# Layer 3's second weights: the third product by quarter blocks too, from the seventh group on, and statistics and first sums placed behind the third's sums

## The chip, the cores and the metric

The kernel runs on one core of one Trainium2 chip. The metric is the device time of one execution in microseconds (us); lower is better. The median of three runs stands for a kernel.

## The reference, cut to what matters

The whole model is four graph layers with a pre-layernorm and a residual on 8192 tokens of width 256 (128 samples of 64 nodes). The change lies in the last one:

```python
# --- layer 3 ---
h = jnp.maximum(_layernorm(x, axis=-1), 0.0)
S = adj
def _slconv(x, adj, S, W):
    support = jnp.einsum('bnf,fh->bnh', x, W)
    return jnp.einsum('nm,bmh->bnh', adj * S, support)
h = relu(_slconv(h, adj, S, W1))   # 256 -> 512
h = relu(_slconv(h, adj, S, W2))   # 512 -> 1024
x = x + _slconv(h, adj, S, W3)     # 1024 -> 256
```

Everything is in float32.

## The kernel before

**Layer 3 by groups.** The tokens are cut into 16 groups of 512 (GT = 4 tiles of 128). For each group g the loop at the end of the kernel goes through these stages: layernorm and the first mixing over the nodes (done ahead, during the group before), `first_weights` (matmuls at L1700), `second_mix` (L146), `second_weights` (L1772 and L197), `third_weights` (L1824), `last_mix` (L1845) and `finish`, which adds to the residual and stores. The stages of neighbouring groups interleave: the last mix of group g-1 and the mixing for g+1 lie between the first and second weights of g. The order of the instructions on each engine is fixed when the program is built; `tc.issue_after(ins)` puts what it traces behind `ins` on the engine of `ins`. Each engine works through its own queue in order, and waits at the head of it.

**Products by seven.** Each weight stage multiplies 2x2 blocks with seven products in place of eight (`seven`): sums of one operand's blocks (`sums`, L339), differences of the other's (`differences`, L327), then products 1, 5, 7, 6 into four PSUM banks. ACT copies products 1 and 5 out (p1, p5; L256), DVE adds 7 and 6, and products 2, 3 and 4 are accumulated into banks that are already in use. The four result blocks are: `out[0][0]` = products 1 + 2; `out[1][1]` = p1 + p5, added by POOL (`last_sum`, L267); `out[0][1]` = p1 + ps[5] with product 3 accumulated into ps[5] (`sum_of_three`, L272); `out[1][0]` = p1 + ps[7] with product 4 accumulated (`sum_of_four`, L278). `end` applies the relu (L350, ACT).

**The second weights** run `seven` in two passes, q = 0 and q = 2, each for two of the four 128-wide column blocks. One product there is four matmuls of 128x128 weights on 256 columns.

**Quarter blocks.** From the fifth group on (`SPLIT_FROM = 4`) products 6 and 2 of both passes are themselves done by seven products of quarter blocks, each one matmul of 128 columns (class `Split`): `first` issues four (1, 5, 7, 6) into the four quarters of one bank, `common` takes them out, `last` accumulates the other three, and `rest` adds three quarters to the target. `common` is

```python
nc.scalar.copy(self.u, q[0])                      # L207, ACT
for k in (1, 2):
    nc.vector.tensor_tensor(t[3], t[3], q[k], ALU.add)          # L209, DVE
summed = nc.vector.tensor_tensor(self.u, self.u, q[3], ALU.add) # L210, DVE
nc.gpsimd.tensor_tensor(out=three, in0=three, in1=self.u...)    # L213, POOL
```

with `u` a 128x128 scratch block in a freed residual tile, one for each split product and shared by the two passes. `rest` is L223 (DVE, 128x384). `split_second` makes the sums of the weights' quarter blocks once, after the fourth group's second weights; `split_differences` (L231) makes those of the activations in each group.

**The order around the change.** The two passes first issue products 1, 5, 7 and the first part of 6 each. Then `half` of pass 1, `half` of pass 2 (product 3, the last part of 6, the first part of 2, and their additions), then `other_half` of each (last part of 2, product 4). The third's sums (L339, four of 128x512 for each of q = 0 and 2) follow on DVE, tied behind `parts_summed` entries (the L210 instructions). The statistics of the group after next (`ln_scale`: L93 to L99, with one POOL instruction at L97) are tied behind the last of the second's differences, that is, they come near the start of the second weights; the next group's first sums (L339, four of 128x256) are free to follow them. What needs the statistics is the rectification on ACT (L112) during the next group's first weights; what needs the first sums is the fifth product there (L1700).

**Tiles.** `arena(ar_right)` hands out eight tiles in rotation; one group uses eight of them.

Of the kernel before, what the change touches and what calls it, by code (L numbers as in the profile page):

```python
# [15 lines left out]
P = 128  # L16
D = 256
# [22 lines left out]
def adj_preln_kernel(ctx: ExitStack, tc: tile.TileContext, x_in, adj, vec, bg0, bg1,  # L40
# [200 lines left out]
    def seven(products, banks, p1, p5, out, end, parts=lambda b: [b], split=None,  # L241
              order=(1, 5, 6, 7)):

        ps = dict(zip(order, banks))
        for i in (1, 5, 7, 6) if split else order:
            if split and i == 6:  # L250
                split[6].first(ps[6])
            else:
                products[i](ps[i], True)
        for i in order:
            if i in (1, 5):
                copied = nc.scalar.copy(p1 if i == 1 else p5, ps[i])  # L256
        if split:
            added = nc.vector.tensor_tensor(p5, p5, ps[7], ALU.add)
            split[6].common(ps[6], p1)
            nc.scalar.copy(out[0][0], ps[1])  # L260
        else:
            nc.vector.tensor_tensor(p1, p1, ps[6], ALU.add)
            added = nc.vector.tensor_tensor(p5, p5, ps[7], ALU.add)  # L263

        def last_sum():
            sums_on_pool.append(
                nc.gpsimd.tensor_tensor(out=out[1][1], in0=p1, in1=p5, op=ALU.add).ins  # L267
            )
            end(1, 1, None)

        def sum_of_three():
            nc.vector.tensor_tensor(out[0][1], p1, ps[5], ALU.add)  # L272
            end(0, 1, None)

        def sum_of_four():
            products[4](ps[7], False)
            for to, p, q in zip(*(parts(b) for b in (out[1][0], p1, ps[7]))):
                last = nc.vector.tensor_tensor(to, p, q, ALU.add)  # L278
                end(1, 0, None, to)
            return last.ins  # L280

        def half():
            products[3](ps[5], False)
            split[6].last(ps[6])
            split[6].rest(ps[6], p1)
            last_sum()
            split[2].first(ps[1])
            split[2].common(ps[1], out[0][0])
            sum_of_three()

        def last_half():
            split[2].last(ps[1])
            split[2].rest(ps[1], out[0][0])
            end(0, 0, None)

        def finish():
            if split:
                half()
                last = sum_of_four()
                last_half()  # L300
                return last
            last_sum()
            products[2](ps[1], False)
            end(0, 0, ps[1])
            products[3](ps[5], False)
            sum_of_three()
            return sum_of_four()

        def other_half():
            last_half()  # L310
            sum_of_four()

        finish.halves = (half, other_half) if split else (finish,)
        finish.behind = added.ins
        finish.copied = copied.ins
        return finish
# [13 lines left out]
    def sums(eng, a11, a12, a21, a22, s1, s2, s3, s4, behind=None, which=range(4)):  # L330

        ops = (
            (s1, a21, a22, ALU.add), (s2, s1, a11, ALU.subtract),
            (s3, a11, a21, ALU.subtract), (s4, a12, s2, ALU.subtract),
        )
        for i in which:
            s, p, q, op = ops[i]
            with each_behind(behind, i):
                last = eng.tensor_tensor(out=s, in0=p, in1=q, op=op)  # L339
        return last.ins  # L340
# [629 lines left out]
    def arena(pool):  # L970
        return pool.tile([P, 4, GN], F32, tag="arena", name="arena")
# [715 lines left out]
        )  # L1687
        return a, lambda: add_back(2, pss[2])

    def first_weights(a, room, copied):  # L1690

        h1 = arena(ar_left)
        act = [[a[:, 2 + c, m * HN : (m + 1) * HN] for c in range(2)] for m in range(2)]
        ss = [a[:, i // 2, (i % 2) * HN : (i % 2 + 1) * HN] for i in range(4)]
        summed = sums(nc.vector, *act[0], *act[1], *ss)

        def product(w, b):
            def issue(ps, first):
                for t in range(2):
                    nc.tensor.matmul(  # L1700
                        ps[:, t, :], lhsT=w[:, t * P : (t + 1) * P], rhs=b,
                        start=first and t == 0, stop=True, skip_group_check=True,
                    )

            return issue

        p1, p5 = (room[:, i, :].rearrange("p (t f) -> p t f", t=2) for i in (2, 3))
        blocks = [[h1[:, 2 * m : 2 * m + 2, n * D : (n + 1) * D] for n in range(2)] for m in range(2)]
        end = seven(
            sevens((*act, ss), (*b1, t1s), product), [bank((P, 2, D)) for _ in range(4)], p1, p5,  # L1710
            blocks, ends_in(blocks, AF.Relu),
        )
        with tc.issue_after(end.copied):
            next_a = copied()
        end()
        return h1, summed, next_a
# [6 lines left out]
            order=[(2, (2, 3, 0, 1)), (0, range(GT))],  # L1723
        )

    def split_second():

        free = [xpool.tile([P, GT, D], F32, tag=f"x{g}", name=f"free{g}") for g in range(3)]
        quarters = {}
        for i, a, s in ((6, s2s[1], free[0]), (2, a2[0][1], free[1])):  # L1730
            rows = a.rearrange("p c (q r f) -> p c r q f", r=2, f=P)
            blocks = [[rows[:, c, r] for c in range(2)] for r in range(2)]
            s = s.rearrange("p a (i f) -> p a i f", f=P)
            split_sums(nc.vector, blocks, s)
            quarters[i] = blocks, s
        return free[2], quarters

    def second_weights(m1, room, within=None):

# [9 lines left out]
        ts = [tt[:, i] for i in range(4)]  # L1749
        last = differences(nc.vector, *act[0], *act[1], *ts)  # L1750
        if within:
            small = within[0].rearrange("p a (i n) -> p (a i) n", n=P)
            tb = {
                6: split_differences(nc.vector, ts[1], small[:, 0:3]),
                2: split_differences(nc.vector, act[1][0], small[:, 3:6]),
            }

        def split(k):
            if not within:
                return None  # L1760
            return {
                i: Split(split_weights(*within[1][i], k), tb[i], small[:, 6 + i // 6])
                for i in (2, 6)
            }

        def products(q):
# [16 lines left out]
        for q in (0, 2):  # L1783
# [7 lines left out]
                    ends_in(blocks, AF.Relu), split=split(q // 2),  # L1791
                )
            )
        for halves in zip(*(end.halves for end in ends)):
            for half in halves:
                half()
        return h2, last

    third_summed = None
# [1 line left out]
    def third_weights(h2, parts=lambda b: [b], split=None):  # L1801
# [12 lines left out]
        nonlocal third_summed  # L1814
        for q in (0, 2):
            act_q, ss_q = ([b[:, q : q + 2] for b in bs] for bs in (act[0] + act[1], ss))
            with behind_parts(-1 if q else -2, split):
                third_summed = sums(nc.vector, *act_q, *ss_q)

        def product(w, b):  # L1820
# [11 lines left out]
        blocks = [[s3[:, 2 * m : 2 * m + 2, n * P : (n + 1) * P] for n in range(2)] for m in range(2)]  # L1832
        seven(
            sevens((*act, ss), (*b3, t3s), product), [bank((P, 2, P)) for _ in range(4)], p1, p5,
            blocks, ends_in(blocks, AF.Copy), parts, order=(5, 1, 6, 7),
        )()
        return s3

# [50 lines left out]
                ready += 1  # L1889

    AHEAD = 4
    SPLIT_FROM = 4
    within = None
    a, finish_start = first_start()
    s3, scaled = None, None
    for g in range(NG + 1):
        if g == 0:
            bring(0, 3)
        if g < NG:

            m1 = arena(ar_right)
            h1, summed, next_a = first_weights(a, m1, lambda: rectified_ahead(g + 1, scaled))
            if g == 0:
                with tc.issue_after(summed):
                    finish_start()
            if g == 0:
                bring(3, 2)
# [19 lines left out]
                mixed_ahead(next_a)  # L1927
            finish(g - 1, pss)
        if g < NG:
            h2, behind = second_weights(m1, h1, within)  # L1930
            if g == SPLIT_FROM - 1:
                with tc.issue_after(behind):
                    within = split_second()
            if g == 0:
                with tc.issue_after(behind):
                    for b, pss in later:
                        add_back(b, pss)
            bring(1, 1, behind)
            if next_a:
                a = next_a  # L1940
            elif g + 1 < NG:
                a = start(g + 1, behind)
            if AHEAD <= g + 2 < NG:
                with tc.issue_after(behind):
                    scaled = ln_scale(xs[g + 2])[:2]
            else:
                scaled = None
            if g == NG - 1:
                s3 = third_weights(h2, lambda b: [b[:, t] for t in range(2)], within)
            else:  # L1950
                s3 = third_weights(h2, split=within if g >= SPLIT_FROM else None)
                if g:
                    bring(1, 1, third_summed)

# [51 lines left out]
```

## Time and profile before

| | before |
|---|---|
| median of 3 runs | 2421.2 us (2419.95 to 2422.31) |
| profiled execution | 2423.3 us |
| its span | 2421.5 us |
| PE busy | 2398.7 us (99%) |
| DVE busy | 1685.4 us (70%) |
| ACT busy | 1177.2 us (49%) |
| POOL busy | 605.9 us (25%) |
| granted TensorE clock | 0.999 |

The profile is of one execution; "span" is from its first to its last instruction. A busy row gives the time in which the engine had an instruction under way. A float32 matmul leaves two records on PE. A row of a timeline gives start, duration, engine, line, operation, tiles and shapes, and in brackets how long the engine was idle before it and who released it. Lines are those of the kernel before.

### The profile page before, as it was taken

How to read it: one execution, taken by the hardware profiler on the slowest of the kernel's cores; microseconds unless marked ns; L12 is line 12 of the kernel's file. 1: busy time of each engine (PE TensorE's matmuls, PEld its weight loads, DVE VectorE, ACT ScalarE, POOL GpSimd, SP SyncE). 2: the span in 40 equal slices, each digit the busy share in tenths (PEclk: the TensorE clock that was granted, in tenths of full speed). 3: DMA queues.
4: the chain of work that ended last, by engine and by line, in shares of the span. 5: the costliest groups of instructions: out<-in, count | busy, mean ns of one | idle time of the engine just before them, and what ended most of it. 6: DMA issues, size and time to landing. Idle time of an engine off the chain costs nothing.

```text
span 2421.5 us, 49124 instructions
## 1 busy us (share of the span) xinstructions
PE 2398.7 (99%) x20272; PEld 2094.3 (86%) x20272; DVE 1685.4 (70%) x3425; ACT 1177.2 (49%) x2178; POOL 605.9 (25%) x549
## 2 busy tenths in 40 slices
PE   9999999999999999999999999999999999999999
PEld 7778888889999999988888867586898999999998
DVE  6768888777566687775599887586556655665664
ACT  4557755555444454453455556564333334333332
POOL 4432222222111112212224444123111311221121
PEclk9999999999999999999999999999999999999999
DMA  4200000001000000053347410010133100000000
GB/s 139 86 2 1 1 18 1 1 1 35 1 1 1 1 1 1 18 127 70 53 78 133 76 32 2 10 62 10 27 62 57 33 10 11 19 10 10 19 10 19
DMA packets 163712, 75.45 MB, mean 31 GB/s; under 512 B 104481, under 2 KB 159905, under 8 KB 163489
## 3 DMA queue, kind: packets, MB, share of 16 engines
q1 hardware_dynamic: 150096, 59.18, 9.8%
q0 software_dynamic: 12672, 12.58, 3.5%
q8 instruction: 159, 2.61, 0.4%
q14 instruction: 65, 0.52, 0.1%
q10 hardware_dynamic: 720, 0.56, 0.1%
HBM read 42.94 MB, written 20.97 MB: 26 GB/s over the span
## 4 chain that ended last, share of the span: by engine, by line
PE 92%; DVE 5%; ACT 2%; issue 1%; POOL 0%; DVEq 0%; ACTq 0%; POOLq 0%
PE ps L704 37%; PE ps L1772 13%; PE ps L1824 8%; PE ps L197 7%; PE ps L1700 4%; PE ps L146 4%; PE ps L1096 3%; PE ps L612 2%; PE ps L638 2%; PE ps L1470 2%; PE ps L1022 2%; PE ps L1055 2%; PE ps L1532 1%; PE ps L1118 1%; PE ps L1845 1%
## 5 line engine op out<-in xcount | busy, mean ns | idle before, releaser
L718 ACT ACTIVATE gates<-gates,lbias 128x512 f32<-128x512 f32 (+3 forms) x482 | 265.7, 605 | 173.7 <-DVE gates L272 121.6
L704 PE MATMUL ps<-diff,s 128*128 128x256 f32 (+1 forms) x1600 | 344.9, 369 | 0.5 <-DVE diff L826 0.5
L704 PEld LDWEIGHTS ps<-diff,s 128*128 128x128 f32 x1600 | 303.3, 190 | 27.5 <-issue 0.9
L1772 PE MATMUL ps<-arena 128*128 128x256 f32 x1408 | 318.5, 380 | 0.0
L267 POOL TENSOR_TENSOR gates<-p 128x512 f32<-128x512 f32 (+1 forms) x115 | 148.9, 1295 | 589.0 <-DVE p L263 518.4
L1772 PEld LDWEIGHTS ps<-arena 128*128 128x128 f32 x1408 | 261.4, 190 | 35.1 <-issue 2.0
L704 PE MATMUL ps<-h,w 128*128 128x256 f32 (+1 forms) x1028 | 242.5, 371 | 0.0
L704 PE MATMUL ps<-diff,w 128*128 128x256 f32 (+1 forms) x1040 | 239.7, 371 | 0.0
L704 PEld LDWEIGHTS ps<-diff,w 128*128 128x128 f32 x1040 | 194.8, 190 | 16.5
L704 PEld LDWEIGHTS ps<-h,w 128*128 128x128 f32 x1028 | 192.7, 190 | 17.7 <-issue 0.5
L267 POOL TENSOR_TENSOR arena<-arena 128x512 f32<-128x512 f32 (+1 forms) x80 | 91.7, 1147 | 461.9 <-DVE arena L263 407.8
L256 ACT COPY p<-ps 128x512 f32<-128x512 f32 (+1 forms) x262 | 142.1, 563 | 60.1 <-PE ps L704 39.7
L350 ACT ACTIVATE arena<-arena 128x512 f32<-128x512 f32 x168 | 98.5, 624 | 121.4 <-POOL arena L267 66.5
L256 ACT COPY arena<-ps 128x512 f32<-128x512 f32 (+1 forms) x160 | 82.2, 517 | 149.6 <-PE ps L1700 59.5
L1824 PE MATMUL ps<-arena 128*128 128x128 f32 x1280 | 149.1, 275 | 0.8 <-DVE arena L339 0.8
L1824 PEld LDWEIGHTS ps<-arena 128*128 128x128 f32 x1280 | 146.7, 192 | 2.1 <-DVE arena L339 1.2
L718 ACT ACTIVATE gates<-ps,lbias 128x256 f32<-128x256 f32 (+2 forms) x157 | 68.2, 479 | 143.9 <-PE ps L704 143.8
L339 DVE TENSOR_TENSOR arena<-arena 128x512 f32<-128x512 f32 (+1 forms) x192 | 111.3, 612 | 29.4 <-ACT arena L350 27.8
L207 ACT COPY free<-ps 128x128 f32<-128x128 f32 x104 | 27.6, 265 | 208.0 <-PE ps L197 208.0
L272 DVE TENSOR_TENSOR gates<-p,ps 128x512 f32<-128x512 f32 (+1 forms) x115 | 76.3, 664 | 65.0 <-PE ps L704 64.2
L704 PE MATMUL ps<-state,s 128*128 128x256 f32 (+1 forms) x512 | 116.3, 370 | 0.6 <-ACT p L256 0.6
L272 DVE TENSOR_TENSOR arena<-arena,ps 128x512 f32<-128x512 f32 (+1 forms) x80 | 48.1, 601 | 87.0 <-PE ps L1824 50.4
(270 smaller groups left out, 4831.0 us busy)
## 6 DMA issues: line engine op xcount, KB each, us to landing
x<-in_x SPq DMA_DIRECT2D x23, 512.0 KB, 4.0
y<-turned SPq DMA_DIRECT2D x64, 128.0 KB, 3.3
v<-vt SPq DMA_DIRECT2D x128, 64.0 KB, 2.6
w<-in_wih SPq DMA_DIRECT2D x4, 1024.0 KB, 7.2
x_for_h<-in_x SPq DMA_DIRECT2D x8, 512.0 KB, 6.9
x<-y POOLq DMA_DIRECT2D x8, 512.0 KB, 6.3
x_for_h<-y POOLq DMA_DIRECT2D x8, 512.0 KB, 6.7
z<-w SPq DMA_DIRECT2D x64, 64.0 KB, 2.0
```

The costliest lines, as they stand in the source:

```text
L146: last = nc.tensor.matmul(pss[b][half * 64 : half * 64 + 64, c, t, :], lhsT=src[rows, t, col : col + 64], rhs=a2[rows, :], start=True, sto ...
L197: nc.tensor.matmul(q[k], lhsT=w, rhs=b, start=first and k == 0, stop=True, skip_group_check=True)
L256: copied = nc.scalar.copy(p1 if i == 1 else p5, ps[i])
L267: nc.gpsimd.tensor_tensor(out=out[1][1], in0=p1, in1=p5, op=ALU.add).ins
L272: nc.vector.tensor_tensor(out[0][1], p1, ps[5], ALU.add)
L339: last = eng.tensor_tensor(out=s, in0=p, in1=q, op=op)
L350: nc.scalar.activation(o, o, func)
L704: nc.tensor.matmul(ps[:, r], lhsT=wc[:, j, :], rhs=bc, start=first and r == 0 and c == 0, stop=True, skip_group_check=True,)
L718: nc.scalar.activation(o, ps, func, bias=lbias[:, col : col + 1])
L1700: nc.tensor.matmul(ps[:, t, :], lhsT=w[:, t * P : (t + 1) * P], rhs=b, start=first and t == 0, stop=True, skip_group_check=True,)
L1772: nc.tensor.matmul(ps[:, r, :], lhsT=w[:, c, col : col + P], rhs=b[:, c, :], start=first and r == 0 and c == 0, stop=c == 1, skip_group_ch ...
L1824: nc.tensor.matmul(ps[:, t, :], lhsT=w[:, c, t * P : (t + 1) * P], rhs=b[:, c, :], start=first and t == 0 and c == 0, stop=c == 3, skip_gr ...
```

## The change

1. From the seventh group on (`SPLIT_MORE_FROM = 6`) product 3 of the second weights is done by quarter blocks too. Its scratch block and differences lie in another freed residual tile, its weight sums in a tile taken from the right arena for good, made after the sixth group's second weights.
2. Where 3 is split, `sum_of_three` adds p1 and ps[5] without the relu; the quarter products are added to that, and the relu follows. The finishing goes in three parts for the two passes in turn: `half`, `third_part`, `fourth_part`. The third part puts the first part of 3 into the bank of product 6.
3. The third weights take product 1 before product 5 where 3 is split.
4. From the fifth group on, the statistics of the group after next and the next group's first sums are tied behind the third's sums. (`third_summed` is the last of these.)

```diff
         def sum_of_three():
             nc.vector.tensor_tensor(out[0][1], p1, ps[5], ALU.add)
-            end(0, 1, None)
+            if not split or 3 not in split:
+                end(0, 1, None)
...
         def half():
-            products[3](ps[5], False)
+            if 3 not in split:
+                products[3](ps[5], False)
             split[6].last(ps[6])
             split[6].rest(ps[6], p1)
             last_sum()
...
-        finish.halves = (half, other_half) if split else (finish,)
+        def third_part():
+            split[3].first(ps[6])
+            last_half()
+            split[3].common(ps[6], out[0][1])
+
+        def fourth_part():
+            split[3].last(ps[6])
+            split[3].rest(ps[6], out[0][1])
+            end(0, 1, None)
+            sum_of_four()
+
+        if not split:
+            finish.parts = (finish,)
+        elif 3 in split:
+            finish.parts = (half, third_part, fourth_part)
+        else:
+            finish.parts = (half, other_half)
...
-    def first_weights(a, room, copied):
+    def first_weights(a, room, copied, behind=None):
...
-        summed = sums(nc.vector, *act[0], *act[1], *ss)
+        with tc.issue_after(behind) if behind else nullcontext():
+            summed = sums(nc.vector, *act[0], *act[1], *ss)
...
-            tb = {
-                6: split_differences(nc.vector, ts[1], small[:, 0:3]),
-                2: split_differences(nc.vector, act[1][0], small[:, 3:6]),
-            }
+            read = {2: act[1][0], 3: act[1][1], 6: ts[1]}
+            order = [i for i in (6, 2, 3) if i in within]
+            small = {}
+            tb = {}
+            for i in order:
+                room_of, k = within[i][2:]
+                small[i] = room_of.rearrange("p a (i n) -> p (a i) n", n=P)[:, 4 * k : 4 * k + 4]
+                tb[i] = split_differences(nc.vector, read[i], small[i][:, 0:3])
...
-            with behind_parts(-1 if q else -2, split):
+            with behind_parts(-1 if q or not split or 3 in split else -2, split):
                 third_summed = sums(nc.vector, *act_q, *ss_q)
...
-            blocks, ends_in(blocks, AF.Copy), parts, order=(5, 1, 6, 7),
+            blocks, ends_in(blocks, AF.Copy), parts,
+            order=(1, 5, 6, 7) if split and 3 in split else (5, 1, 6, 7),
...
-    SPLIT_FROM = 4
+    SPLIT_FROM, SPLIT_MORE_FROM = 4, 6
...
+            h1, summed, next_a = first_weights(
+                a, m1, lambda: rectified_ahead(g + 1, scaled), third_summed if split_now else None
+            )
...
+            if g == SPLIT_MORE_FROM - 1:
+                to = arena(ar_right).rearrange("p a n -> p (a n)")
+                with tc.issue_after(behind):
+                    within = split_second(
+                        dict(within), (3,), freed(3), [to[:, : 2 * GN]]
+                    )
...
-            if AHEAD <= g + 2 < NG:
+            scaled = None
+            if AHEAD <= g + 2 < NG and not split_now:
                 with tc.issue_after(behind):
                     scaled = ln_scale(xs[g + 2])[:2]
...
-                s3 = third_weights(h2, split=within if g >= SPLIT_FROM else None)
+                s3 = third_weights(h2, split=split_now)
+                if split_now and g + 2 < NG:
+                    with tc.issue_after(third_summed):
+                        scaled = ln_scale(xs[g + 2])[:2]
```

More of the change, by code (lines that the diff above doesn't have):

```diff
@@ L1724, in second_mix, with split_second, freed @@
         )
[L1726 to L1731, printed above, removed]
-            blocks = [[rows[:, c, r] for c in range(2)] for r in range(2)]
[L1733 to L1736, printed above, removed]
+    def split_second(within, which, room_of, sums_in):
+        weights = {2: a2[0][1], 3: s2s[3], 6: s2s[1]}
+        for k, (i, to) in enumerate(zip(which, sums_in)):
+            rows = weights[i].rearrange("p c (q r f) -> p c r q f", r=2, f=P)
+            blocks = [[rows[:, c, r] for c in range(2)] for r in range(2)]
+            to = to.rearrange("p (i k f) -> p i k f", i=4, f=P)
+            split_sums(nc.vector, blocks, to)
+            within[i] = blocks, to, room_of, k
+        return within
+    def freed(g):
+        return xpool.tile([P, GT, D], F32, tag=f"x{g}", name=f"free{g}")
     def second_weights(m1, room, within=None):
@@ L1751, in second_weights @@
         if within:
-            small = within[0].rearrange("p a (i n) -> p (a i) n", n=P)
-            tb = {
-                6: split_differences(nc.vector, ts[1], small[:, 0:3]),
-                2: split_differences(nc.vector, act[1][0], small[:, 3:6]),
-            }
+            read = {2: act[1][0], 3: act[1][1], 6: ts[1]}
[6 more added lines that the diff above has]
+                tb[i] = split_differences(nc.vector, read[i], small[i][:, 0:3])
         def split(k):
@@ L1761, in split @@
             return {
-                i: Split(split_weights(*within[1][i], k), tb[i], small[:, 6 + i // 6])
-                for i in (2, 6)
+                i: Split(split_weights(*within[i][:2], k), tb[i], small[i][:, 3]) for i in order
             }
@@ L1793, in second_weights @@
             )
-        for halves in zip(*(end.halves for end in ends)):
-            for half in halves:
-                half()
+        for both in zip(*(end.parts for end in ends)):
+            for part in both:
+                part()
         return h2, last
@@ L1891, in adj_preln_kernel @@
     AHEAD = 4
-    SPLIT_FROM = 4
+    SPLIT_FROM, SPLIT_MORE_FROM = 4, 6
     within = None
     a, finish_start = first_start()
-    s3, scaled = None, None
+    s3, scaled, split_now = None, None, None
     for g in range(NG + 1):
@@ L1901, in adj_preln_kernel @@
             m1 = arena(ar_right)
-            h1, summed, next_a = first_weights(a, m1, lambda: rectified_ahead(g + 1, scaled))
+            h1, summed, next_a = first_weights(
+                a, m1, lambda: rectified_ahead(g + 1, scaled), third_summed if split_now else None
+            )
             if g == 0:
@@ L1929, in adj_preln_kernel @@
         if g < NG:
-            h2, behind = second_weights(m1, h1, within)
+            split_now = within
+            h2, behind = second_weights(m1, h1, split_now)
             if g == SPLIT_FROM - 1:
                 with tc.issue_after(behind):
-                    within = split_second()
+                    to = [freed(i).rearrange("p a d -> p (a d)") for i in range(2)]
+                    within = split_second({}, (6, 2), freed(2), to)
+            if g == SPLIT_MORE_FROM - 1:
[4 more added lines that the diff above has]
+                    )
             if g == 0:
@@ L1942, in adj_preln_kernel @@
                 a = start(g + 1, behind)
-            if AHEAD <= g + 2 < NG:
+            scaled = None
+            if AHEAD <= g + 2 < NG and not split_now:
                 with tc.issue_after(behind):
                     scaled = ln_scale(xs[g + 2])[:2]
-            else:
[L1947 to L1950, printed above, removed]
-                s3 = third_weights(h2, split=within if g >= SPLIT_FROM else None)
+            if g == NG - 1:
+                s3 = third_weights(h2, lambda b: [b[:, t] for t in range(2)], split_now)
+            else:
+                s3 = third_weights(h2, split=split_now)
+                if split_now and g + 2 < NG:
+                    with tc.issue_after(third_summed):
+                        scaled = ln_scale(xs[g + 2])[:2]
                 if g:
```

## The prediction

> **What bounds the kernel now.** The page's first part comes first: TensorE (PE) works for 99% of the span, the others far less.
>
> ```profile
> PE 2398.7 (99%) x20272; PEld 2094.3 (86%) x20272; DVE 1685.4 (70%) x3425; ACT 1177.2 (49%) x2178; POOL 605.9 (25%) x549
> ```
>
> So only two things count: how much PE has to do, and whether PE has to wait. The windows view, cut at the starts of the groups of layer 3, says this for the ninth group (span, then busy time of PE, PEld, DVE, ACT, POOL, clock and DMA):
>
> ```profile
> 2055.82:2101.91 46.09, 46.09 (x486) 42.63 (x485) 28.10 (x68) 17.77 (x35) 9.71 (x9) 1.00 0.04 13
> ```
>
> PE fills all 46.09 us at full clock. DVE works 28 us and POOL under 10, but in bursts; what matters is the burst around the change. The chain of waits in order of time (start, us, what; a matmul leaves two records, so x8 is four matmuls) shows it:
>
> ```profile
> 2067.27 0.89 PE ps L197 x8
> 2068.16 1.73 PE ps L1772 x8
> 2069.89 1.56 PE ps L197 x14
> 2071.45 1.73 PE ps L1772 x8
> 2073.18 2.23 PE ps L197 x20
> 2075.41 1.73 PE ps L1772 x8
> 2077.14 0.67 PE ps L197 x6
> 2077.81 1.73 PE ps L1772 x8
> 2079.54 12.50 PE ps L1824 x112
> ```
>
> The two L1772 rows at 2068.16 and 2071.45 are the third product of the two passes (q = 0 and 2). They are work, and they are also time in which the other engines finish their part of products six and two. POOL's timeline in that stretch:
>
> ```profile
> 2069.51 0.99 POOL L213 TENSOR_TENSOR arena<-arena,free 128x384 f32<-128x384 f32 x1 [2.28 <-DVE free L210]
> 2071.30 1.29 POOL L267 TENSOR_TENSOR arena<-arena 128x512 f32<-128x512 f32 x1 [0.80 <-DVE arena L223]
> 2072.68 1.01 POOL L213 TENSOR_TENSOR arena<-arena,free 128x384 f32<-128x384 f32 x1
> 2075.04 1.30 POOL L267 TENSOR_TENSOR arena<-arena 128x512 f32<-128x512 f32 x1 [1.36 <-DVE arena L223]
> 2076.89 1.01 POOL L213 TENSOR_TENSOR arena<-arena,free 128x384 f32<-128x384 f32 x1 [0.54 <-DVE free L210]
> ```
>
> and DVE's just before the end of product two's common part in pass 2:
>
> ```profile
> 2075.60 0.28 DVE L209 TENSOR_TENSOR arena<-arena,ps 128x128 f32<-128x128 f32 x1
> 2075.80 0.55 DVE L223 TENSOR_TENSOR arena<-arena,ps 128x384 f32<-128x384 f32 x1
> 2076.27 0.28 DVE L209 TENSOR_TENSOR arena<-arena,ps 128x128 f32<-128x128 f32 x1
> 2076.46 0.28 DVE L210 TENSOR_TENSOR free<-free,ps 128x128 f32<-128x128 f32 x1
> ```
>
> That L210 ends at 2076.74; PE writes the same bank again (last quarter products of two, pass 2) at 2077.14. The slack of the tightest place is 0.40 us.
>
> **Part 1: fewer PE cycles.** In ten groups (seventh to sixteenth) each pass gives up one 1.73 us product (four 128x256 matmuls) for seven 128x128 ones, 1.56 us by the x14 row. That is 0.17 us a pass, 0.34 a group, 3.4 us in all. It is on the path, since PE is.
>
> **Part 2: work added beside PE, per group.** ACT: two L207 copies of 0.27. DVE: per pass two L209, one L210 (0.20 from start to start) and one L223 (0.47), 2.14 for both, plus four 128x128 differences of 0.20: 2.9 us. POOL: two L213, 2.0 us. On totals DVE goes to about 31 of 46 us and POOL to under 12, so no engine becomes the bound. The block sums made once after the sixth group's products are four 128x256 adds, 0.31 each, in a group where DVE is idle for 19 us: nothing on the path, 1.2 us if that idle time were gone. The arena on the right loses one tile of eight for good; when the next group's first tile is wanted (first eviction at 2092.95) the mixed tile and the differences' tile have been dead since 2079.54, so I take no wait, and 0.2 us a group as the upper bound.
>
> **Part 3: the order in the stretch.** The build shows the new order. PE: last of six and first of two for pass 1, the same for pass 2, then first of three and last of two for pass 1, first of three for pass 2, half of product four, and only then last of two for pass 2. POOL: L213 (six, pass 2), then both L267 one behind the other, then L213 (two, pass 1), where before L267 and L213 took turns. The scratch block u of a split product is one tile for both passes. So ACT's copy L207 of pass 2 may not write it before POOL's L213 of pass 1 has read it; that L213 now stands behind two additions of 1.29.
>
> Worked on the group above, from 2068.16:
> - PE: 0.67 + 0.89 + 0.67 + 0.89 + 0.89 + 0.67 + 0.89 + 0.86 (half of 1.73) = 6.43; it wants last of two, pass 2, at 2074.59.
> - POOL: L213 ends 2070.50 as before. Back to back with 0.09 between (as from 2072.59 to 2072.68): L267 to 2071.88, L267 to 2073.26, L213 2073.35 to 2074.35. Their inputs are there: the two L223 follow PE's 2068.83 and 2070.39 by about a microsecond.
> - ACT copies at 2074.38 for 0.27. DVE then runs the four rows shown above (the build has the same four in the same order), 1.14 us from start to end: 2074.67 to 2075.81.
> - PE waits from 2074.59 to about 2075.83: **1.2 us**.
>
> The same again for product three, whose u is also shared. PE: last of two and last of three, 0.67 each, about 0.05 of wait, then two halves of product four, 1.73, so it wants last of three, pass 2, at 2078.95. POOL: L213 (two, pass 2) starts 0.15 behind the L210, 2075.96, ends 2076.97; L213 (three, pass 1) 2077.06 to 2078.07; copy to 2078.37; four DVE rows to 2079.53. **0.6 us**.
>
> Then the third weights. Their first product now needs no sum; the next needs s1, which needs product three's relu. PE gets there at 2079.55 + 0.67 + 0.86 + 1.79 = 2082.87. Rest L223, relu (0.6), an addition queued ahead on DVE (0.6) and the sum itself (0.7) from 2080.25 on end at about 2082.8 to 2083.2. I take 0.15 us, with 0 and 0.5 as ends.
>
> Sum for a group: 1.2 + 0.05 + 0.6 + 0.15 - 0.34 = +1.65 us; ten groups, +16.5 us.
>
> A row on contention: the two L339 at 2077.56 beside POOL's L213 took 1.48 us, the two at 2080.03 beside an idle POOL 1.28. The Trainium skill (GPSIMD Engine Reference, Key points) says why this could speak against the change: GpSimd shares its SBUF interfaces with VectorE and contends with instructions that read two SBUF inputs. By it the third's sums beside the added L213 would cost another 0.2 a group, and the sum would be +18.5 us. I keep 1.65, since the four DVE rows that set the two large waits read PSUM; the 0.2 us by which the two rows differ goes into the range.
>
> **Part 4: statistics and first sums moved.** L93 to L99 and the four 128x256 L339 go from the start of the group (2060.44 to 2064.7) to behind the third's sums, already from the fifth group on. Queued behind them on DVE are the third product's additions (L262), on POOL behind the 1.12 us L97 its L267; the rectification by ACT that needs them stands at 2094.29, the first weights at 2092.04. They end near 2090, so nothing waits: 0, and at most 0.5 a group if the third's sums come later than worked out. The gain is that the quarter differences and the first L213 come some 3 us sooner, where PE did not wait: 0 as well.
>
> **From the trace to the time.** The profiled execution took 2423.3 us, its span 2421.5, the median of the runs is 2421.2. The sum makes it 2439.8 for such an execution; at the median 2421.2 + 16.5 = 2437.7, said as 2437.
>
> **Rivals.** (a) POOL does not hold PE up: it would be so if L213 (two, pass 1) were done 1.2 us earlier, at 2073.1, as it would with the old alternation. Then only part 1 is left, 2421.2 - 3.4 = 2417.8: not slower, and inside 0.2% (4.8 us, about what a measurement of this kernel can tell from no change). For it: today the stretch has no wait at all. Against it: the slack is 0.40 and PE comes 2.55 us earlier. Chance 6%. (b) The same, and PE's pauses named "issue" in the mixes (3.7 us in four places from 1860 on, by the view of waits) go too, because the instruction stream shifts: 2414.1, faster. Nothing in the diff aims at them. 2%. (c) Only the first wait bites, the second and third are covered: +1.2 - 0.34 = 0.86 a group, 2429.8. 12%. (d) DVE is late as well (contention 0.2, sums 0.35 more): 2.2 a group, 2443. 12%.
>
> **How the numbers follow.** The forecast proper has 68%, with 2432 to 2441 as its own range (0.3 to 0.5 us a group either way). Adding (c) and most of (d): 2429 to 2443. Slower by over 0.2%: 92%; within: 6%; faster: 2%.
>
> **What would show it.** Right: the third-product rows L1772 x8 gone in ten groups, group spans of 47.5 to 48, PE idle 1 us and 0.5 us ahead of L197 with DVE as releaser, ACT's L207 waiting for POOL's addition to the three quarters, and POOL running two L267 back to back. Wrong: group spans of 45.75 (rival a), or waits that sit at the third or first weights instead. Groups five and six should keep their time.

## The result, and the profile after

The changed kernel takes 2441.74 us (median of 4 runs, 2440.06 to 2442.86) against 2421.76 us of the kernel before on the same chip: a ratio of 1.0081, with a 95% interval of 1.0067 to 1.0094. It is slower, by 20.0 us at the medians and by 18.7 us between the two profiled spans (2440.2 and 2421.5). The forecast was 2437, with 2429 to 2443 as its range.

The first part of the page after:

```profile
PE 2403.6 (99%) x20392; PEld 2095.3 (86%) x20392; DVE 1717.0 (70%) x3549; ACT 1184.1 (49%) x2198; POOL 625.9 (26%) x569
```

PE's records say 99% again. The ends of these records are modelled, so busy time shows waits inside a burst of matmuls only in part; the length of a group shows them whole. The windows view of a later group after the change (tenth group; columns as before):

```profile
2107.92:2155.85 47.93, 46.69 (x509) 42.82 (x505) 31.07 (x81) 18.49 (x38) 11.65 (x11) 1.00 0.04 12
```

47.93 us against 46.09, so +1.84 a group where +1.65 was worked out. PE's busy column shows only 1.24 us of this group as idle (47.93 less 46.69). Ten groups at 1.84 are 18.4 us. From the start of the seventh group to the end the profiled executions differ by 19.4 us (477.3 against 457.9): PE's pauses named "issue", 0.6 to 1.2 us each, fall in other groups in the two, and up to the seventh group the changed one was 0.7 us ahead. DVE and POOL are where part 2 of the forecast put them (31.07 and 11.65), and the clock stays at 1.00 through the waits.

The chain of waits in that group (start, us, what) names the mechanism:

```profile
2123.49 2.56 POOL arena L267 x2
2126.05 0.97 POOL arena L213
2127.01 0.02 issue
2127.04 0.27 ACT free L207
...
2127.54 0.55 DVE arena L223
2128.09 0.20 DVE arena L209
2128.28 0.21 DVE free L210
2128.49 0.14 issue
2128.63 1.62 PE ps L197 x12
```

Before, this stretch was PE rows alone. Now the path runs through POOL (two `last_sum` additions, then the addition that frees u), ACT's copy, the four DVE rows and back to PE. PE's own timeline there has the sizes (the change moved L1772 to L1795, L1824 to L1847, L339 to L357, L278 to L279 and L350 to L368):

```profile
2126.62 1.03 PE L1795 MATMUL ps<-arena 128*128 128x256 f32 x4
2128.63 0.46 PE L197 MATMUL ps<-arena 128*128 128x128 f32 x2 [0.97 <-DVE free L210]
...
2130.09 1.89 PE L1795 MATMUL ps<-arena 128*128 128x256 f32 x8
2132.20 0.68 PE L197 MATMUL ps<-arena 128*128 128x128 f32 x4 [0.22 <-DVE free L210]
...
2133.80 5.96 PE L1847 MATMUL ps<-arena 128*128 128x128 f32 x48
2139.61 1.95 PE L1847 MATMUL ps<-w,arena 128*128 128x128 f32 x16
```

Read from start to start: four records of L1795 are 0.86 us of work, so PE was free at 2127.48 and started at 2128.63, a wait of 1.15. Eight records are 1.73, free at 2131.82, start at 2132.20: 0.38. The first 48 records of the third weights take 5.81 us to the next row, where they took 5.36 before (1987.20 to 1992.56 in the seventh group): 0.45 of waits inside them. (The expectations below put this third wait at 0.6. That figure counts from a start in PE's timeline to one in the chain, and the starts in the chain of a PE that does not wait lie 0.16 us later.) Small ones behind the two restarts add 0.2: twelve records from 2128.63 take 1.46 for 1.34 of work, six from 2132.20 take 0.74 for 0.67. Together these are 2.18, and 0.34 less work leaves the 1.84.

### The profile page after: what moved, and what is told of

It reads as the page before. It is cut to its first block, busy times and chain, and to the rows that moved or that the text cites. A ratio compares the mean times of both kernels' runs of the same rounds, so it can differ in the third digit from the quotient of the medians.

```text
span 2440.2 us, 49619 instructions
## 1 busy us (share of the span) xinstructions
PE 2403.6 (99%) x20392; PEld 2095.3 (86%) x20392; DVE 1717.0 (70%) x3549; ACT 1184.1 (49%) x2198; POOL 625.9 (26%) x569
## 4 chain that ended last, share of the span: by engine, by line
PE 86%; DVE 8%; ACT 2%; POOL 2%; issue 2%; DMA 0%; DVEq 0%; ACTq 0%; POOLq 0%
PE ps L722 37%; PE ps L1795 10%; PE ps L1847 7%; PE ps L197 5%; PE ps L1719 4%; PE ps L146 4%; PE ps L1114 3%; PE ps L630 2%; PE ps L656 2%; PE ps L1488 2%; PE ps L1040 2%; PE ps L1073 2%; PE ps L1550 1%; PE ps L1136 1%; DVE arena L357 1%
## 5 line engine op out<-in xcount | busy, mean ns | idle before, releaser
L1795 PE MATMUL ps<-arena 128*128 128x256 f32 x1248 | 282.3, 381 | 0.7 <-issue 0.7
L1795 PEld LDWEIGHTS ps<-arena 128*128 128x128 f32 x1248 | 231.8, 190 | 32.1 <-issue 2.6
L368 ACT ACTIVATE arena<-arena 128x512 f32<-128x512 f32 x168 | 102.7, 628 | 125.1 <-POOL arena L267 69.9
L1847 PE MATMUL ps<-arena 128*128 128x128 f32 x1280 | 152.9, 277 | 1.3 <-DVE arena L357 0.8
L1847 PEld LDWEIGHTS ps<-arena 128*128 128x128 f32 x1280 | 148.2, 192 | 5.0 <-DVE arena L357 3.6
L213 POOL TENSOR_TENSOR arena<-arena,free 128x384 f32<-128x384 f32 x68 | 68.1, 1008 | 241.1 <-DVE free L210 241.0
L357 DVE TENSOR_TENSOR arena<-arena 128x512 f32<-128x512 f32 (+1 forms) x196 | 114.3, 621 | 6.7 <-ACT arena L368 6.2
```

Of the source, the lines that this page charges most:

```text
L368: nc.scalar.activation(o, o, func)
L1795: nc.tensor.matmul(ps[:, r, :], lhsT=w[:, c, col : col + P], rhs=b[:, c, :], start=first and r == 0 and c == 0, stop=c == 1, skip_group_ch ...
L1847: nc.tensor.matmul(ps[:, t, :], lhsT=w[:, c, t * P : (t + 1) * P], rhs=b[:, c, :], start=first and t == 0 and c == 0, stop=c == 3, skip_gr ...
```

## The experiments

Theory A is that of the forecast: product 3 by quarters puts `last_sum` of both passes back to back on POOL ahead of the addition that reads u, u is shared by the passes, and PE waits for the copy into it. Rival B: the stretch is simply too dense for DVE and POOL, whatever the order. Rival C: the moved statistics and first sums cost it. Group lengths are from start to start of the second weights in the chain of waits, in groups without other pauses of PE.

**1. Own scratch for the second pass** (`e1_own_scratch`)

```diff
-                i: Split(split_weights(*within[i][:2], k), tb[i], small[i][:, 3]) for i in order
+                i: Split(
+                    split_weights(*within[i][:2], k), tb[i],
+                    spare[:, 4 + i % 4] if k and 3 in within and i in (2, 3) else small[i][:, 3],
+                )
+                for i in order
```

(`k` is 1 in the second pass; `spare` is the fourth freed tile, cut into blocks of 128 columns.)

> The changed kernel, but products 2 and 3 have a scratch block u for each pass (pass 2 in unused quarters of the fourth freed tile). Theory A (ACT's copy into the shared u waits for POOL's queue, and PE for the copy): the waits of 1.14 and 0.38 us ahead of the last parts of 2 and 3, pass 2, shrink to at most 0.5 together and the third's wait of 0.6 goes with them, since its sums come earlier: group 46.0 to 46.5 us instead of 47.94, time 2422 to 2427. Rival B (the added work is simply too dense for DVE and POOL, 31 and 11.7 us a group): the group stays above 47.3, time above 2435. Rival C (the moved statistics and first sums cost it): nothing changes, 2441.7.

Measured: 2426.15 us against 2422.32, ratio 1.0012 (1.0003 to 1.0022); group 46.33. The same instructions on the same engines, only another address for u, and 1.6 us of the 1.84 are gone. Rivals B and C fall as explanations of the bulk. What is left is seen in ACT's timeline of this kernel:

```profile
2121.61 0.63 ACT L368 ACTIVATE arena<-arena 128x512 f32<-128x512 f32 x1 [1.76 <-POOL arena L267]
2122.15 0.25 ACT L207 COPY free<-ps 128x128 f32<-128x128 f32 x1
```

The copy no longer depends on POOL, but it stands behind a relu that does: a wait at the head of a queue holds what is behind it. What this costs by itself was not measured: the fifth experiment moves the relu together with POOL's order.

**2. POOL's additions alternate again** (`e2_alternate`)

```diff
-            sums_on_pool.append(
-                nc.gpsimd.tensor_tensor(out=out[1][1], in0=p1, in1=p5, op=ALU.add).ins
-            )
+            with tc.issue_after(parts_pooled[-1]) if split and 3 in split else nullcontext():
+                sums_on_pool.append(
+                    nc.gpsimd.tensor_tensor(out=out[1][1], in0=p1, in1=p5, op=ALU.add).ins
+                )
```

(`parts_pooled` holds POOL's additions of u.)

> The changed kernel, with u still shared, but POOL's addition last_sum of pass 2 is tied behind its addition of product 2, pass 1, so that L267 and L213 alternate as they did before. Theory A: the reading of u comes one L267 (1.29 us) earlier, so the first wait (1.14) goes; the second stays at 0.4 to 0.5 and the third's at 0.4 to 0.6: group 46.6 to 47.0, time 2428 to 2432. Rival B: the same work in the same window, group stays above 47.5, time above 2437. Rival C: 2441.7.

Measured: 2431.25 us, ratio 1.0035 (1.0023 to 1.0047); group 46.69. The timeline of POOL in this kernel, where the two additions stood together before:

```profile
2119.24 1.29 POOL L269 TENSOR_TENSOR arena<-arena 128x512 f32<-128x512 f32 x1
2120.50 1.00 POOL L213 TENSOR_TENSOR arena<-arena,free 128x384 f32<-128x384 f32 x1
2121.46 1.30 POOL L269 TENSOR_TENSOR arena<-arena 128x512 f32<-128x512 f32 x1
```

The order alone is worth 1.25 us a group: the first wait, as sized. The other two stay (0.39 and 0.44 us on PE's timeline).

**3. The statistics and first sums put back** (`e3_statistics_back`)

```diff
-                a, m1, lambda: rectified_ahead(g + 1, scaled), third_summed if split_now else None
+                a, m1, lambda: rectified_ahead(g + 1, scaled)
...
-            if AHEAD <= g + 2 < NG and not split_now:
+            if AHEAD <= g + 2 < NG:
...
-                if split_now and g + 2 < NG:
-                    with tc.issue_after(third_summed):
-                        scaled = ln_scale(xs[g + 2])[:2]
```

> The changed kernel without the two ties behind the third's sums: the statistics are tied behind the second's differences and the first sums are free, as before the change; product 3 stays split. Theory A: both lie where PE does not wait, so 2441.7 within 2 us and the group at 47.9. Rival C: the time goes back by more than 4 us, towards 2422 if they are the whole loss.

Measured: 2441.33 us, ratio 1.0078 (1.0063 to 1.0093); group 47.94. Nothing comes back.

**4. The ties alone** (`e4_ties_alone`)

```diff
-    SPLIT_FROM, SPLIT_MORE_FROM = 4, 6
+    SPLIT_FROM, SPLIT_MORE_FROM = 4, NG + 1
```

> The two ties alone, from the fifth group on; product 3 is never split. Theory A: 2421.8 within 2 us and the group at 46.1. Rival C: slower than before by more than 4 us. If the ties help by themselves (first additions of POOL come 3 us sooner): at most the pauses that PE shows in no wait, so 2418 at the lowest.

Measured: 2423.39 us against 2422.32, ratio 1.0003 (0.9993 to 1.0013); group 46.09. With the third experiment this closes rival C: the ties cost nothing and bring nothing that can be measured.

**5. All three repairs** (`e5_all_three`): own scratch, alternation, and the relu of `out[1][1]` tied behind ACT's copies.

```diff
         def last_sum():
...
-            end(1, 1, None)
+            if not split or 3 not in split:
+                end(1, 1, None)
...
         def fourth_part():
+            with tc.issue_after(u_copied[-1]):
+                end(1, 1, None)
```

> Product 3 split as in the change, with three repairs: own scratch blocks for pass 2 (first experiment), POOL's additions alternating (second), and the relu of out[1][1], which waits for POOL, tied on ACT behind the copies of product 3 in place of standing ahead of them. Theory A: no wait of PE above 0.1 us in the stretch and none at the third weights, so the group falls to 45.75 (46.09 less 0.34) and the time to 2422.3 - 3.4 = 2419, a ratio of 0.9986 to before. Rival B (density of DVE and POOL): waits of 0.3 us a group or more remain and the time is not below 2422.

Measured: 2420.26 us against 2422.21 (11 and 15 runs), ratio 0.9991 with an interval of 0.9982 to 1.0000; group 45.82. PE's timeline in the stretch has no bracket, that is, no idle time, down to the third weights:

```profile
2122.55 1.03 PE L1809 MATMUL ps<-arena 128*128 128x256 f32 x4
2123.42 0.61 PE L199 MATMUL ps<-arena 128*128 128x128 f32 x4
...
2125.62 1.89 PE L1809 MATMUL ps<-arena 128*128 128x256 f32 x8
2127.35 5.56 PE L1861 MATMUL ps<-arena 128*128 128x128 f32 x48
```

0.27 us a group shorter than before, where 0.34 was the work saved: the product by quarters is worth its price once nothing waits. The gain of 2 us lies at the edge of what these runs resolve. Rival B is closed too: the same DVE and POOL work fits. The tile given up on the right and the new order of the third's products (points 1 and 3 of the change) are no cause either, since this kernel keeps both.

**6. Own scratch for product 2 alone** (`e6_own_scratch_two`): as the first, with `i in (2,)`.

> The changed kernel with a scratch block for each pass for product 2 alone; product 3's stays shared. Theory A: the first wait (1.14 us) shrinks to 0.3, the second stays or grows (0.4 to 0.8, POOL now is one L213 behind it), and a little of the third: group 46.7 to 47.2, time 2430 to 2434. If the first wait does not shrink, the shared scratch is not its cause.

Measured: 2432.47 us, ratio 1.0042 (1.0028 to 1.0055); group 47.01. The idle time ahead of the first wait's L197 falls from 0.97 to 0.28 us, so the shared scratch is its cause. Product 2's block is worth 0.9 us a group and product 3's the other 0.7 (46.33 in the first experiment).

**7. Product 3's shared addition on VectorE** (`e7_three_on_vector`)

```diff
-            nc.gpsimd.tensor_tensor(
+            (nc.vector if dve else nc.gpsimd).tensor_tensor(
                 out=three, in0=three, in1=self.u.unsqueeze(1).to_broadcast([P, 3, self.h]),
```

(with `dve` true for product 3)

> The changed kernel, but the addition of u to three quarters of product 3 (L213) runs on VectorE, so POOL has no instruction beside the third's sums; the scratch of product 2 stays shared. Theory A with the contention: the first wait stays at 1.1 to 1.2, the second goes, and so does the wait at the third weights (0.6), since the first sum of the third no longer runs beside POOL and takes 0.68 us again in place of 1.11: group 46.8 to 47.1, time 2430 to 2434. If the wait at the third weights came from DVE's load alone, it would stay at 0.6 or grow, as DVE gets two more additions: group above 47.4, time above 2436.

Measured: 2432.68 us, ratio 1.0043 (1.0028 to 1.0059); group 47.03. The first wait stays and everything behind it goes, although DVE got two more additions. It does not separate the contention from the second wait, which went with it. Nor did it change DVE and POOL alone: in this build PE takes the third's products in another order, and where the changed kernel waits, behind some 24 records, two matmuls on weights from `w` stand in between:

```profile
2129.56 2.84 PE L1847 MATMUL ps<-arena 128*128 128x128 f32 x24
2132.24 0.61 PE L1847 MATMUL ps<-w,arena 128*128 128x128 f32 x4
```

The next experiment keeps that order and separates the contention.

**8. POOL kept busy beside the third's sums** (`e8_pool_beside_sums`): the kernel of the fifth experiment and

```diff
             split[3].common(ps[6], out[0][1])
+            beside.append(0)
+            if len(beside) % 2 == 0:
+                w = extra_room[0]
+                for i in range(2):
+                    with tc.issue_after(parts_pooled[-1]):
+                        nc.gpsimd.tensor_tensor(
+                            out=w[:, 2 * GN + 384 * i : 2 * GN + 384 * (i + 1)], in0=w[:, 0:384], in1=w[:, 384:768],
+                            op=ALU.add,
+                        )
```

(Every second call is the second pass; `extra_room` holds the tile of product 3's weight sums.)

> The kernel of the fifth experiment (all three repairs) with two more 128x384 additions on POOL in each of the ten groups, tied behind product 3's addition of pass 2, so that POOL is busy while VectorE makes the third's first sums. Their result goes to an unused half of a tile and nobody reads it. Contention theory: the third's first sum, which reads two SBUF inputs, holds until POOL's instruction ends and takes 1.1 to 1.4 us in place of 0.68; the additions that read PSUM keep their 0.68; PE then waits 0.4 to 0.8 us at the third weights, group 46.2 to 46.6 in place of 45.82, time 2424 to 2428. Without contention: POOL's work has no reader, so all durations and the group stay, time 2420.

Measured: 2426.15 us against 2422.16, ratio 1.0016 (1.0006 to 1.0026); group 46.53, 0.7 more than without. DVE's timeline (L375 are the third's sums, L228 and L286 read PSUM):

```profile
2125.37 0.69 DVE L286 TENSOR_TENSOR arena<-arena,ps 128x512 f32<-128x512 f32 x1 [0.24 <-PE ps L1820]
2125.98 1.06 DVE L375 TENSOR_TENSOR arena<-arena 128x512 f32<-128x512 f32 x1
2126.96 0.54 DVE L228 TENSOR_TENSOR arena<-arena,ps 128x384 f32<-128x384 f32 x1
2127.42 1.02 DVE L375 TENSOR_TENSOR arena<-arena 128x512 f32<-128x512 f32 x1
```

and POOL's and PE's in the same place:

```profile
2125.48 2.41 POOL L331 TENSOR_TENSOR arena<-arena 128x384 f32<-128x384 f32 x2
```

```profile
2130.90 2.94 PE L1872 MATMUL ps<-arena 128*128 128x128 f32 x24 [0.49 <-DVE arena L375]
```

Work that nobody reads makes a group 0.7 us longer (the bracket, up to modelled ends, shows 0.49 of it), because two DVE instructions with two SBUF inputs took 1.06 and 1.02 us beside it in place of 0.68, 0.72 together. The PSUM readers kept their times.

## Why the prediction was right, point by point

- **Part 1** (0.34 us a group of PE work saved): the fifth experiment shows 0.27 in the length of a group.
- **First wait**, worked out at 1.2: 1.15. Its cause is shown twice, by the address of u (experiments 1 and 6) and by POOL's order (2). That the size agrees so closely is partly luck. Counted from the start of the group, POOL's addition for pass 1 ended 0.38 us sooner than worked out (18.15 for 18.53; its records follow each other without the 0.09 that was put between them), PE came back 0.15 behind the L210 and not 0.02, and PE wanted the product 0.14 sooner, since the working counted from a start in the chain. These errors nearly cancel.
- **Second wait**, worked out at 0.6: 0.38. The working had PE go on 0.02 us behind the L210 of product 2 and POOL 0.15; in the trace PE too came back 0.15 us behind it (2128.49 to 2128.63) and so wanted the next product later, and POOL's two additions took 1.95 us in place of 2.11.
- **Third wait**, worked out at 0.15 with 0.5 as its upper end: 0.45. This term was too small, because the contention was left out of the sum. The forecast's row on contention had it at 0.2 for a pair that overlapped POOL for only a third of a microsecond; here POOL's last addition lies across most of the first sum:

```profile
2132.13 1.00 POOL L213 TENSOR_TENSOR arena<-arena,free 128x384 f32<-128x384 f32 x1 [1.55 <-DVE free L210]
```

```profile
2132.57 1.11 DVE L357 TENSOR_TENSOR arena<-arena 128x512 f32<-128x512 f32 x1
```

  The sum started 0.44 us after POOL's addition and ended 0.55 us behind its end, as if it had not begun before; 0.43 us are lost, and the sum that PE waits for is behind it (PEld is the loading of weights), with no idle time of DVE in between:

```profile
2136.60 2.53 PEld L1847 LDWEIGHTS ps<-arena 128*128 128x128 f32 x22 [0.24 <-DVE arena L357]
```

  The Trainium skill (SBUF — State Buffer, section "SBUF: two separate sides") says what kind of sharing this is: a DVE instruction with two SBUF inputs and a GpSimd instruction that reads SBUF exclude each other for the whole instruction, and whichever starts first goes first. The eighth experiment agrees in both directions: each L375 ended 0.55 us behind POOL's addition (2126.49 and 2127.89), and POOL's two additions, which would have been 2.0 us, took 2.41. The forecast named this contention but priced it by a row with little overlap, as if it were a fixed cost. That row fits as well: its first L339, from 2077.56, took 0.88 us and ended 0.54 behind POOL's L213 (2077.90). Contention is not the only way to a third wait: in the sixth experiment no sum stood beside POOL and 0.19 us were left (5.54 us for the 48 records).
- **The sum**, +1.65 a group: 1.84. It is nearer than its terms, which is luck too: the second wait was put 0.2 us too long, the third 0.3 and the small ones 0.15 too short.
- **Part 4** (statistics and first sums free of charge): shown by experiments 3 and 4.
- **One miss outside the sum.** The sums of the weights' blocks, made once in the sixth group, were put at nothing because DVE is idle for 19 us there. They were queued inside the dense stretch instead, beside POOL (one of them took 0.89 us where 0.31 was reckoned), and PE waited once:

```profile
1936.83 0.46 PE L197 MATMUL ps<-arena 128*128 128x128 f32 x2 [0.82 <-DVE free L210]
```

  PE had been free 0.98 us before that, at 1935.85, so the 1.2 us named as the price without cover was about right; the sixth group did not keep its time.
- **Rivals.** (a), the case without waits, needed the alternation on POOL, as it said; by itself that brings only the first wait back, and the kernel that reached 45.82 has the private scratch and the relu's new place as well. (b) fell: the chain after still has PE pauses of 0.65 to 1.03 us. (c), the first wait alone, fell: the two others are 0.8 us together. (d), DVE late as well, had the right kind of cost, but the second wait came out smaller, so the group is 1.84 us longer and not 2.2.

## What to carry to other kernels

An engine with a quarter of its time busy can hold up one that is full: what counts is how many of its instructions stand between two that the full engine needs, and here a product that was removed had also been the time in which they ran. When work is cut from the bound engine, list what was hidden beside it, look for scratch that two passes share and for instructions that wait at the head of a queue, and give the second pass its own scratch first, where an unused block allows it: here it changed one address and brought back 1.6 of 1.84 us. A cheaper product may be right and still lose until those waits are gone.

## What the runs showed of the hardware that had not been expected

A DVE addition with two SBUF inputs does not run slowly beside a POOL addition; it stands until POOL's instruction ends (0.55 us from there to its own end, in the changed kernel and in the eighth experiment), and POOL stands for it in turn. In the four rows measured here the loss is the overlap less 0.13 to 0.14 us (0.34, 0.47, 0.51 and 0.56 us of overlap cost 0.20, 0.34, 0.38 and 0.43). Additions that read one operand from PSUM are untouched (0.54 and 0.69 us beside POOL). So a POOL instruction that nobody waits for still has a price where DVE makes sums of two SBUF tiles.
